# Cross attention in seven-product blocks: values formed with channels on the partitions and turned afterwards, and query tiles of every fourth column

## The chip, the cores and the metric

The kernel runs on one core of one Trainium2 chip. The metric is the device time of one launch in microseconds. TensorE multiplies, and has two rows in the profile: PE for the products and PEld for the loads of their stationary operand. VectorE (DVE), ScalarE (ACT) and GpSimd (POOL) do the elementwise work. SyncE (SP) issues transfers, and GpSimd issues those that add to what lies in SBUF.

## The reference

```
x: (32, 256, 1024)   y = ctx: (32, 256, 1024)   C = 256, N = 1024, float32
x_q = w_qk y (turned), x_k = w_qk x, x_v = w_v x + b_v
energy    = x_q x_k                       # (N queries, N keys)
attention = softmax(energy, over keys)
attention = attention / (1e-7 + attention.sum(over queries))
x_r = x_v attention                       # contracted over the queries' index n
out = x + relu(w_t (x - x_r) + b_t)
```

Since both projections use `w_qk`, the energy is y' (w_qk' w_qk) x. Since `w_t` is applied to `x_r`, the kernel folds it into the values: u = -(w_t w_v) x - w_t b_v, and what is left for the output is w_t x + u attention + b_t.

## The kernel before, in words

All products are float32, and each product of 2 by 2 blocks is done with seven block products instead of eight. A block of the moving operand has 512 columns. The class `Seven` holds the frame: products `p1`, `p5`, `p2`, `p6`, `p3`, `p7`, `p4` in three PSUM banks (`one`, `two`, `three`), with partial sums copied out by ScalarE (`kept`), and four results `c11`, `c12`, `c22`, `c21` made by VectorE (`combine`) or, for `c21`, mostly by ScalarE. Three products lie in the same bank one on another, so `p6` waits for the copy of `p1`, `p7` for the copy `w` of `p6`, and `p4` for `c22`, which reads the bank before.

For each of the 32 batches there are four such objects.

- `Keys`: gx, the matrix w_qk' w_qk times x. Seven products of 512 columns.
- `Values`: u, turned, with n on the partitions and the 256 channels along a row (`ut`). The seven products each are four of 128 columns: a tile of 128 columns of x is stationary and 128 columns of weights move.
- `Energy`, for t = 0 to 3: queries of tile t are stationary (128 columns of y), gx moves (512 columns). The result is a tile of e with the queries on the partitions. ScalarE takes the exponential (`exp`), VectorE adds the normalized rows up in `acc` (`share`).
- `Attention`: the output, po. Seven products with the weights and x (`xpart`), and seven of four each that contract over n (`epart`): tiles of `ut` and of its sums `us` are stationary, normalized e and its sums `et` move.

So 70 products of 512 columns and 28 of 128 make a batch on TensorE. The names of the traces follow: pg, pu, pe and po are the banks of the four objects.

The sums of blocks that the seven products need are made by GpSimd (`gt` from gx, `us` from `ut`, in `factors`) and, for x and y, by transfers that add (`summed`; its three steps are issued on GpSimd's queue, each waiting for the one before). The bias of the values is a transfer too: `Values.bias` adds `uc`, spread over all rows, to the whole of `ut`.

The order on each engine is the order written in the program: `InOrder` chains every instruction of an engine behind the one before, which is why all of them have line 77. SP's queue is in the order of the program too. The loop over the batches runs them overlapped:

1. Energy tiles t = 0 to 3 of batch b. Within t = 0 stands the rest of the batch before: its last product (`before.end()`: `xpart` and `epart` 4), then `before.c21()`, which is an activation on ScalarE into a buffer `z`, an addition on VectorE and a store. On ScalarE that activation stands between the copies of `p5` and `p6` of tile 0. The sums `us` of batch b are started here, then the next x is loaded and, at t = 1 to 3, its sums.
2. While tile 3 drains: `Keys` and `Values` of batch b + 1, the column sums and their inverse `rc`.
3. `Attention` of batch b (`begin`, `run`): VectorE normalizes 16 half tiles of e (`normal`), makes the sums et (`mix`) and the results. `run` ends with `c12`. Then products 7, `c22`, two `put` (relu, addition of x, store), and round again.

The results go through the buffers `z`, of which there are two: `c11`, `c12`, `c22` and `c21` take them in turn, so that `c22` waits for the store of `c11`, and `c21` for the store of `c12`.

Of the kernel before, what the change touches and what calls it, by code (L numbers as in the profile page):

```python
# [9 lines left out]
F32 = mybir.dt.float32  # L10
# [6 lines left out]
def kernel(  # L17
# [48 lines left out]
    class InOrder:  # L66


        def __init__(self, engine):
            self.engine = engine  # L70
            self.last = None
# [37 lines left out]
    def accumulate(into, from_):  # L109
        return pool.dma_start(into, from_, accum_op=ALU.add)  # L110
# [13 lines left out]
    bv = scratch[:, 4, :KC].rearrange("p (k o) -> p k o", o=1)  # L124
    bt = const.tile([P, KC, 1], F32, name="bt")
    nbt = const.tile([P, KC, 1], F32, name="nbt")
    uc = const.tile([P, 1, C], F32, name="uc")
    nc.sync.dma_start(wqk, w_qk.rearrange("(k p) c -> p k c", p=P))
    load("x", 0, KC)
    nc.sync.dma_start(wt, w_t.rearrange("(k p) c -> p k c", p=P))  # L130
# [7 lines left out]
    few = const.tile([P, P], F32, name="few")  # L138
    dve.memset(few, 0.0)
    dve.memset(zeros, 0.0)  # L140
    parts = const.tile([P, NB, NG + 1], F32, name="parts")
    dve.memset(parts[:, :, NG], EPS)
    idle = bank("idle")
# [41 lines left out]
    def value_weights(wtT):  # L185

        pw = [bank(f"pw_{i}") for i in range(KC)]
        for i in range(KC):
            for k in range(KC):
                pe.matmul(  # L190
                    pw[i][:, :C], wv[:, k, ts(i, P)], wtT[:, k, :], start=(k == 0), stop=(k == KC - 1)
                )
        return lefts("wvtT", pw, -1.0)[1]

    bvb = scratch[:, 6, : KC * P].rearrange("p (k c) -> p k c", k=KC)

    def spread_bias():
        for k in range(KC):
            act.activation(bvb[:, k, :], few, AF.Identity, bias=bv[:, k, :], scale=1.0)

    def value_bias(wtT):

        pb = bank("pb")
        for k in range(KC):
            pe.matmul(
                pb[:, :C], bvb[:, k, :], wtT[:, k, :], start=(k == 0), stop=(k == KC - 1)
            )
        act.mul(uc[:, 0, :], pb[:, :C], -1.0)
        act.mul(nbt[:, :, 0], bt[:, :, 0], -1.0)

    up = ctx.enter_context(tc.tile_pool(name="up", bufs=2))
# [7 lines left out]
    def matmul(into, lhs, rhs, onto=False):  # L219
        pe.matmul(into, lhs, rhs, start=not onto, stop=True, skip_group_check=onto)  # L220
# [114 lines left out]
    class Values(Seven):  # L335


        def __init__(self, b, xr):
            super().__init__("u", b)
            self.xr = xr  # L340
            self.ut = up.tile([P, NT, C], F32, tag="ut", name=f"ut_{b}")

        def product(self, into, j, onto=False):
            for t in range(HT):
                pe.matmul(
                    into[:, ts(t, P)],
                    self.xr[j - 1][:, ts(t, P)],
                    u_left[j - 1],
                    start=(t == 0 and not onto),
                    stop=(t == HT - 1),  # L350
                    skip_group_check=True,
                )

        def tiles(self, p):
            return p.rearrange("p (t c) -> p t c", t=HT)

        def block(self, i, h):
            return self.ut[:, h * HT : h * HT + HT, ts(i, P)]

        def combine(self, i, h, in0, in1, op):  # L360
            dve.tensor_tensor(self.block(i, h), self.tiles(in0), self.tiles(in1), op)

        def c21(self):
            act.copy(self.block(1, 0), self.tiles(self.one))

        def bias(self):
            accumulate(self.ut, uc.to_broadcast([P, NT, C]))

        def factors(self):

            us = up.tile([P, 4, HT, P], F32, tag="us", name=f"us_{self.b}")
            s1, s2, s3, s4 = (us[:, j] for j in range(4))
            a11, a12, a21, a22 = (self.block(i, h) for i in range(2) for h in range(2))
            steps = [
                lambda: pool.tensor_tensor(s1, a21, a22, ALU.add),
                lambda: pool.tensor_tensor(s2, s1, a11, ALU.subtract),
                lambda: pool.tensor_tensor(s3, a11, a21, ALU.subtract),
                lambda: pool.tensor_tensor(s4, a12, s2, ALU.subtract),
            ]
            return (a11, a12, s4, a22, s1, s2, s3), steps  # L380

    class Energy(Seven):

# [6 lines left out]
            self.ends = {}  # L390

        def product(self, into, j, onto=False):
            matmul(into, self.rhs[j - 1][:, ts(self.t, P)], self.lhs[j - 1], onto)

        def combine(self, i, h, in0, in1, op):

# [42 lines left out]
    class Attention(Seven):  # L439
# [76 lines left out]
        def run(self, u, before=None):  # L516


            self.normal(0, 0)
            self.normal(1, 0)  # L520
            for j in range(HT // 2):
                self.normal(0, 1, j)
                self.mix(self.t1, self.b11, self.b12, ALU.add, j)
            if u:
                u.c22()
            if before:
                before.put()
                before.c21()
            self.normal(1, 1)
            self.mix(self.t2, self.t1, self.b22, ALU.subtract)  # L530
            self.epart(self.one, 1)
            self.p1s = self.biased(self.one, "p1s", bt[:, 0, :])
            self.epart(self.three, 2)
            self.epart(self.two, 5)
            self.p5s = self.biased(self.two, "p5s", bt[:, 1, :])
            self.xpart(self.one, 6, True)
            if u:
                u.p4()
                u.c21()
                u.c11()  # L540
                u.c12()
            self.c11()
            self.put()
            self.xpart(self.two, 3, True)
            self.epart(self.two, 3, (0, 1))
            self.epart(self.one, 6)
            self.w = self.biased(self.one, "w", nbt[:, 0, :])
            self.mix(self.t3, self.b12, self.b22, ALU.subtract)
            self.mix(self.t4, self.b21, self.t2, ALU.subtract)
            self.epart(self.two, 3, (2,))  # L550
            if u:
                self.epart(self.two, 3, (3,))
                self.c12()

        def end(self):
            self.xpart(self.one, 4, True)
# [57 lines left out]
    g.c11()  # L614
    g.p6()
    wtT, t_left = turned_weights()
    spread_bias()
    g.p3()
    g.c12()
    g.p7()  # L620
    g.c22()
    u_left = value_weights(wtT)
    g.p4()
    g.c21()
    rhs, _ = summed("y", 0)
# [6 lines left out]
    u = Values(0, xr)  # L632
    u.p1()
    u.p5()
    value_bias(wtT)
    u.p2()
    u.c11()
    u.p6()
# [6 lines left out]
    for b in range(B):  # L645
# [3 lines left out]
        for t in range(HT):  # L649
            now = Energy(b, t, lhs, rhs)  # L650
            pair.append(now)
            now.p1()
            if t > 0:
                pair[t - 1].exp(1)
            now.p5()
            if t == 0:
                if b == 0:
                    u.p4()
                    u.c21()
                    u.bias()  # L660
                    xsteps[1]()
                    xsteps[2]()
                elif more:
                    before.end()
                    before.c21()
                    load("x", b + 1)
                e = ep.tile([P, NT, N], F32, tag="e", name=f"e_{b}")
                acc = one.tile([P, N], F32, tag="acc", name=f"acc_{b}")
                ur, usteps = u.factors()
                first = 1 if more else 0  # L670
                for step in usteps[:first] + gsteps + usteps[first:]:
                    step()
            if t > 1:
                pair[t - 2].share(0)
            if t == 0:
                now.p6()
            now.p2()
            now.c11()
            if t == 1:
                pair[0].scale(1)  # L680
            if t > 1:
                pair[t - 1].share(1)
            if t > 0:
                now.p6()
            if t == 1:
                act.activation(acc, e[:, HT, :], AF.Copy, scale=scales[HT])
            if t > 0:
                pair[t - 1].p4()
                pair[t - 1].c21()
                pair[t - 1].exp(0)  # L690
            now.p3()
            now.c12()
            now.p7()
            now.c22()
            if more and b > 0:
                if t == 0:
                    xn, xsteps = summed("x", b + 1)
                else:
                    xsteps[t - 1]()
# [49 lines left out]
        if more:  # L749
            now = Attention(b, xr, ur)  # L750
            now.begin()
            ysteps[0]()
            now.run(un)
            if b + 2 < B:
                now.xpart(now.one, 7, True)
                now.epart(now.one, 7)
                now.c22()
                now.put()
            now.put()
            ysteps[1]()  # L760
            un.bias()
            ysteps[2]()
            before = now
            xr, u = xn, un
        else:
            before.end()
            now.run(None, before)
            now.finish()
# [30 lines left out]
```

## Time and profile before

| | |
|---|---|
| Median of 3 runs | 2141.96 us (2141.42 to 2142.52) |
| The profiled execution | 2142.63 us, its span 2140.9 us |
| PE busy | 2134.6 us (100%), PEld 1058.5 us (49%) |
| DVE busy | 1769.1 us (83%) |
| ACT, POOL busy | 788.5 us (37%), 612.7 us (29%) |
| Chain that ended last | PE 98%, DVE 2% |
| Products of the values (pu) | 1792 rows, 32 x 7 x 4 x 2 |
| Store of a result z | 343 ns on SP, 2.3 us from issue to landing (median) |
| Transfer that adds the bias | 32 x 1024 KB, 9.6 us from issue to landing |

A row of the timeline gives the start, the busy time, the engine, the operation and, in brackets, how long the engine had been idle and what it waited for. A float32 product shows as two rows of MATMUL and two of LDWEIGHTS. The modelled ends of products overlap, so the time of one is the distance of two starts. The batches repeat: the third store of the three of one group leads the next group by the same distance each time, and the stretch from 700 to 780 us of the span is used below for all.

### The profile page before, as it was taken

The numbers are of one execution on the slowest core, as the hardware profiler recorded it, in microseconds if no ns is written. First come the engines' busy times: TensorE is split into PE (matmuls) and PEld (weight loads), VectorE is DVE, ScalarE is ACT, GpSimd is POOL, SyncE is SP. The second block draws the span as 40 slices with busy tenths as digits, with TensorE's granted clock in tenths as the row PEclk, the third lists the DMA queues.
The fourth block names the chain that finished last, engine by engine and source line by source line (L and its number), as shares of the span: only waits on it lengthen the run. The fifth ranks groups of instructions, "written<-read, shape, count | busy, mean of one in ns | idle before, by whom it ended". The sixth has DMA issues, their size and how long they took to land.

```text
span 2140.9 us, 19900 instructions
## 1 busy us (share of the span) xinstructions
PE 2134.6 (100%) x6312; PEld 1058.5 (49%) x6312; DVE 1769.1 (83%) x3119; ACT 788.5 (37%) x1323; POOL 612.7 (29%) x488
## 2 busy tenths in 40 slices
PE   9999999999999999999999999999999999999999
PEld 5455444554445545455544555445554445544453
DVE  5889788898788887879878788778897888978898
ACT  5234443244432344333443234442244422444332
POOL 5322323313233133232232322323223233222320
PEclk9999999999999999999999999999999999999999
DMA  6555665556665556665566655665546655566540
GB/s 176 120 127 119 154 151 123 129 120 150 148 126 135 117 144 148 128 151 106 137 151 138 139 113 128 157 144 126 125 121 153 157 121 125 121 154 148 123 98 30
DMA packets 139048, 282.58 MB, mean 132 GB/s; under 512 B 9152, under 2 KB 42688, under 8 KB 138944
## 3 DMA queue, kind: packets, MB, share of 16 engines
q0 software_dynamic: 75936, 114.83, 34.0%
q1 hardware_dynamic: 63008, 166.48, 23.5%
q8 instruction: 50, 0.82, 0.2%
q14 instruction: 54, 0.44, 0.1%
HBM read 181.67 MB, written 33.55 MB: 101 GB/s over the span
## 4 chain that ended last, share of the span: by engine, by line
PE 98%; DVE 2%; issue 0%; DVEq 0%
PE po L77 44%; PE pe L77 35%; PE pu L77 9%; PE pg L77 9%; DVE e L77 1%; DVE acc L77 0%; PE idle L77 0%; DVE et L77 0%; PE pw L77 0%; DVE z L77 0%; DVE rc L77 0%; DVE sc L77 0%; PE pb L77 0%; DVE ri L77 0%; DVE parts L77 0%
## 5 line engine op out<-in xcount | busy, mean ns | idle before, releaser
L77 PE MATMUL pe<-gt,ys 128*128 128x512 f32 x768 | 392.1, 592 | 0.0
L77 DVE SCALAR_TENSOR_TENSOR e<-e,ri,rc 128x512 f32<-128x512 f32 x512 | 347.3, 745 | 1.1
L77 PE MATMUL po<-et,us 128*128 128x512 f32 x768 | 345.7, 593 | 0.5 <-DVE et L77 0.5
L77 DVE SCALAR_TENSOR_TENSOR acc<-e,ri,acc 128x1024 f32<-128x1024 f32 x224 | 288.6, 1288 | 8.0
L77 PE MATMUL pe<-gx,y 128*128 128x512 f32 x512 | 261.4, 592 | 0.0
L77 PEld LDWEIGHTS po<-et,us 128*128 128x128 f32 x768 | 145.5, 190 | 185.0 <-issue 166.8
L77 PEld LDWEIGHTS pe<-gt,ys 128*128 128x128 f32 x768 | 145.8, 190 | 183.4 <-issue 170.0
L77 PE MATMUL po<-e,ut 128*128 128x512 f32 x512 | 224.9, 592 | 0.0
L77 POOL TENSOR_TENSOR gt<-gx 128x512 f32<-128x512 f32 x64 | 81.6, 1274 | 391.4 <-DVE gx L77 391.4
L77 ACT COPY ep1s<-pe 128x512 f32<-128x512 f32 x128 | 75.0, 586 | 303.4 <-PE pe L77 298.9
L77 ACT ACTIVATE e<-e,nm 128x1024 f32<-128x1024 f32 x128 | 147.1, 1149 | 98.2 <-DVE nm L77 96.7
L77 DVE TENSOR_TENSOR et<-e 128x1024 f32<-128x1024 f32 x128 | 156.8, 1246 | 2.3
L77 PEld LDWEIGHTS po<-e,ut 128*128 128x128 f32 x512 | 97.3, 190 | 122.5 <-issue 106.2
L77 PEld LDWEIGHTS pe<-gx,y 128*128 128x128 f32 x512 | 97.2, 190 | 122.0 <-issue 114.1
L77 POOL TENSOR_TENSOR us<-ut 128x512 f32<-128x512 f32 x64 | 87.0, 1360 | 223.9 <-DMA ut<-uc 223.9
L77 ACT ACTIVATE e<-e,bias 128x1024 f32<-128x1024 f32 x128 | 147.4, 1152 | 1.6 <-DVE bias L77 1.5
L77 POOL DMA_DIRECT2D ut<-uc x32 | 50.5, 1579 | 338.0 <-DVE ut L77 281.1
L77 DVE TENSOR_TENSOR z<-z,x 128x512 f32<-128x512 f32 x31 | 46.3, 1492 | 118.3 <-ACT z L77 118.3
L77 DVE CUSTOM_DVE_ANT_0 e<-pe,ep1s 128x512 f32<-128x512 f32 x128 | 88.1, 688 | 64.2 <-ACT e L77 57.8
L77 PE MATMUL pe<-gx,ys 128*128 128x512 f32 x256 | 130.9, 593 | 0.5 <-DVE nm L77 0.5
L77 PE MATMUL pe<-gt,y 128*128 128x512 f32 x256 | 130.8, 592 | 0.0
L77 PE MATMUL po<-e,us 128*128 128x512 f32 x256 | 120.5, 592 | 0.0
(115 smaller groups left out, 3265.5 us busy)
## 6 DMA issues: line engine op xcount, KB each, us to landing
y<-in_ctx_dram SPq DMA_DIRECT2D x32, 1024.0 KB, 5.0
ut<-uc POOLq DMA_DIRECT2D x32, 1024.0 KB, 9.6
out_dram<-z SPq DMA_DIRECT2D x128, 256.0 KB, 2.3
x<-in_x_dram SPq DMA_DIRECT2D x31, 1024.0 KB, 6.2
xs<-in_x_dram SPq DMA_DIRECT2D x62, 512.0 KB, 4.6
ys<-in_ctx_dram SPq DMA_DIRECT2D x62, 512.0 KB, 4.2
xs<-in_x_dram POOLq DMA_DIRECT2D x31, 512.0 KB, 8.1
xs<-xs POOLq DMA_DIRECT2D x31, 512.0 KB, 5.0
```

Source lines behind the costliest of these rows:

```text
L77: self.last = getattr(self.engine, name)(*args, **kwargs)
```

## The change

The values are made with channels on the partitions: the weights are stationary, and 512 columns of x move, as for the keys. Their bias is now one number for each partition and is added where ScalarE copies partial sums (`bu` and its negative `nbu`); the transfer that added `uc` is gone. `ut` then holds u unturned, and `turn` turns it: VectorE transposes four tiles of 128 x 512 in blocks of 32 x 32, reading every fourth element (n = 4 k + t) and writing every fourth, and sixteen transfers on SP's queue, each of 32 partitions by 4 pieces of 512 bytes, move the blocks to their partitions, back into `ut`. `turn` stands at the end of `run`, behind `c12`.

Since n = 4 k + t, tile t of the values, and so of e, has every fourth n. The queries of an energy tile and the stationary tiles of `ut` and `us` are now read with a step of four elements. `us` is one row of 512 instead of four of 128. On GpSimd a copy of one element, `behind`, comes first in t = 0; it waits for the last sum `et` of the batch before. Then come the two sums `gt`, then the four `us`; before, the first `us` came ahead of the `gt`. The four small products for the bias move from the values of the first batch to the weights.

```diff
     def value_bias(wtT):
 
         pb = bank("pb")
-        for k in range(KC):
-            pe.matmul(
-                pb[:, :C], bvb[:, k, :], wtT[:, k, :], start=(k == 0), stop=(k == KC - 1)
-            )
-        act.mul(uc[:, 0, :], pb[:, :C], -1.0)
+        for i in range(KC):
+            for k in range(KC):
+                pe.matmul(
+                    pb[:, i : i + 1],
+                    wtT[:, k, ts(i, P)],
+                    bv[:, k, :],
+                    start=(k == 0),
+                    stop=(k == KC - 1),
+                )
+        act.mul(nbu[:, :, 0], pb[:, :KC], 1.0)
+        act.mul(bu[:, :, 0], pb[:, :KC], -1.0)
         act.mul(nbt[:, :, 0], bt[:, :, 0], -1.0)
...
     class Values(Seven):
...
-            self.ut = up.tile([P, NT, C], F32, tag="ut", name=f"ut_{b}")
+            self.ut = up.tile([P, KC, MH, MB], F32, tag="ut", name=f"ut_{b}")
 
         def product(self, into, j, onto=False):
-            for t in range(HT):
-                pe.matmul(
-                    into[:, ts(t, P)],
-                    self.xr[j - 1][:, ts(t, P)],
-                    u_left[j - 1],
-                    start=(t == 0 and not onto),
-                    stop=(t == HT - 1),
-                    skip_group_check=True,
-                )
+            matmul(into, u_left[j - 1], self.xr[j - 1], onto)
+
+        def bias(self, tag):
+            return {"p1s": bu[:, 0, :], "w": nbu[:, 0, :], "p5s": bu[:, 1, :]}[tag]
+
+        def kept(self, p, tag):
+            s = temp(tag, f"u{tag}_{self.b}")
+            act.activation(s, p, AF.Identity, bias=self.bias(tag), scale=1.0)
+            return s
...
-            act.copy(self.block(1, 0), self.tiles(self.one))
-
-        def bias(self):
-            accumulate(self.ut, uc.to_broadcast([P, NT, C]))
+            act.activation(self.block(1, 0), self.one, AF.Identity, bias=bu[:, 1, :], scale=1.0)
+
+        def turn(self):
+            turned = one.tile([P, KC * MH, NG, P], F32, tag="turned", name=f"turned_{self.b}")
+            for i in range(KC):
+                for h in range(MH):
+                    dve.transpose(
+                        turned[:, i * MH + h].rearrange("p g (c t) -> p g t c", t=HT),
+                        self.block(i, h).rearrange("p (g k t) -> p g t k", g=NG, t=HT),
+                    )
+            to = self.ut.rearrange("p i h (a c) -> p (i h) a c", a=NG)
+            for a in range(NG):
+                for g in range(NG):
+                    nc.sync.dma_start(to[ts(g, G32), :, a, :], turned[ts(a, G32), :, g, :])
 
         def factors(self):
-            us = up.tile([P, 4, HT, P], F32, tag="us", name=f"us_{self.b}")
+            us = up.tile([P, 4, MB], F32, tag="us", name=f"us_{self.b}")
...
-            return (a11, a12, s4, a22, s1, s2, s3), steps
+            return [
+                f.rearrange("p (c t) -> p t c", t=HT)
+                for f in (a11, a12, s4, a22, s1, s2, s3)
+            ], steps
...
     class Energy(Seven):
...
         def product(self, into, j, onto=False):
-            matmul(into, self.rhs[j - 1][:, ts(self.t, P)], self.lhs[j - 1], onto)
+            queries = self.rhs[j - 1].rearrange("p (k t) -> p t k", t=HT)[:, self.t]
+            matmul(into, queries, self.lhs[j - 1], onto)
...
             if u:
                 self.epart(self.two, 3, (3,))
                 self.c12()
+                u.turn()
...
                 if b == 0:
                     u.p4()
                     u.c21()
-                    u.bias()
+                    u.turn()
...
                 ur, usteps = u.factors()
-                first = 1 if more else 0
-                for step in usteps[:first] + gsteps + usteps[first:]:
+                if before is not None:
+                    pool.tensor_copy(behind, before.t4[:, HT - 1, :1])
+                for step in gsteps + usteps:
                     step()
...
             ysteps[1]()
-            un.bias()
             ysteps[2]()
```

More of the change, by code (lines that the diff above doesn't have):

```diff
@@ L126 @@
     nbt = const.tile([P, KC, 1], F32, name="nbt")
-    uc = const.tile([P, 1, C], F32, name="uc")
+    bu = const.tile([P, KC, 1], F32, name="bu")
+    nbu = const.tile([P, KC, 1], F32, name="nbu")
     nc.sync.dma_start(wqk, w_qk.rearrange("(k p) c -> p k c", p=P))
@@ L140 @@
     dve.memset(zeros, 0.0)
+    behind = const.tile([P, 1], F32, name="behind")
     parts = const.tile([P, NB, NG + 1], F32, name="parts")
@@ L193, in value_weights @@
         return lefts("wvtT", pw, -1.0)[1]
-    bvb = scratch[:, 6, : KC * P].rearrange("p (k c) -> p k c", k=KC)
-    def spread_bias():
-        for k in range(KC):
-            act.activation(bvb[:, k, :], few, AF.Identity, bias=bv[:, k, :], scale=1.0)
     def value_bias(wtT):
         pb = bank("pb")
-        for k in range(KC):
-            pe.matmul(
-                pb[:, :C], bvb[:, k, :], wtT[:, k, :], start=(k == 0), stop=(k == KC - 1)
-            )
-        act.mul(uc[:, 0, :], pb[:, :C], -1.0)
+        for i in range(KC):
[9 more added lines that the diff above has]
+        act.mul(bu[:, :, 0], pb[:, :KC], -1.0)
         act.mul(nbt[:, :, 0], bt[:, :, 0], -1.0)
@@ L354, in tiles @@
-        def tiles(self, p):
-            return p.rearrange("p (t c) -> p t c", t=HT)
+            matmul(into, u_left[j - 1], self.xr[j - 1], onto)
[5 more added lines that the diff above has]
+            return s
         def block(self, i, h):
-            return self.ut[:, h * HT : h * HT + HT, ts(i, P)]
+            return self.ut[:, i, h]
@@ L360, in combine @@
         def combine(self, i, h, in0, in1, op):
-            dve.tensor_tensor(self.block(i, h), self.tiles(in0), self.tiles(in1), op)
+            dve.tensor_tensor(self.block(i, h), in0, in1, op)
         def c21(self):
-            act.copy(self.block(1, 0), self.tiles(self.one))
-        def bias(self):
-            accumulate(self.ut, uc.to_broadcast([P, NT, C]))
+            act.activation(self.block(1, 0), self.one, AF.Identity, bias=bu[:, 1, :], scale=1.0)
[11 more added lines that the diff above has]
+                    nc.sync.dma_start(to[ts(g, G32), :, a, :], turned[ts(a, G32), :, g, :])
@@ L616 @@
     wtT, t_left = turned_weights()
-    spread_bias()
     g.p3()
@@ L622 @@
     u_left = value_weights(wtT)
+    value_bias(wtT)
     g.p4()
@@ L634 @@
     u.p5()
-    value_bias(wtT)
     u.p2()
```

## The prediction

> **What bounds the kernel now.** I read the page's busy shares and the chain that ended last first, then the timeline of one batch, engine by engine, then the groups by shape.
>
> The page says TensorE throughout:
>
> ```profile
> PE 2134.6 (100%) x6312; PEld 1058.5 (49%) x6312; DVE 1769.1 (83%) x3119; ACT 788.5 (37%) x1323; POOL 612.7 (29%) x488
> ...
> PE 98%; DVE 2%; issue 0%; DVEq 0%
> ```
>
> The timeline of TensorE gives the price of each kind:
>
> ```profile
> 1113.38 1.02 PE L77 MATMUL pg<-xs,gs 128*128 128x512 f32 x2
> 1114.23 1.05 PE L77 MATMUL pu<-wvtT,x 128*128 128x128 f32 x8
> 1115.12 1.06 PE L77 MATMUL pu<-wvtTs,xs 128*128 128x128 f32 x8
> 1116.02 1.06 PE L77 MATMUL pu<-wvtT,x 128*128 128x128 f32 x8
> ```
>
> Start to start, a product of 512 columns takes 0.859 us (0.429 a row) and four of 128 take 0.894. A batch is 70 x 0.859 + 7 x 0.894 = 66.39 us. The stores of six batches repeat every 66.34. So TensorE fills the batch, but the other engines run close behind it. That shows around the end of a batch, first on VectorE:
>
> ```profile
> 712.98 0.75 DVE L77 CUSTOM_DVE_ANT_0 e<-pe,zeros,nm 128x512 f32<-128x512 f32 x1
> ...
> 745.76 0.68 DVE L77 TENSOR_TENSOR z<-po,ow 128x512 f32<-128x512 f32 x1
> 749.28 0.69 DVE L77 TENSOR_TENSOR z<-op5s,po 128x512 f32<-128x512 f32 x1 [2.83 <-PE po L77]
> 749.88 2.35 DVE L77 SCALAR_TENSOR_TENSOR z<-z,x 128x512 f32<-128x512 f32 x2
> 756.01 1.58 DVE L77 TENSOR_TENSOR z<-z,x 128x512 f32<-128x512 f32 x1 [3.77 <-ACT z L77]
> ```
>
> The first line is the result of the last energy product, and that product started on PE at 711.92 and ended by 712.78: no slack. From there to c12 (745.76) VectorE has no idle time. Only behind c12 are there 2.83 us. Then ScalarE, TensorE and SP in the same place:
>
> ```profile
> 755.29 0.69 ACT L77 ACTIVATE z<-po,bt 128x512 f32<-128x512 f32 x1 [3.65 <-PE po L77]
> 756.14 0.59 ACT L77 COPY ew<-pe 128x512 f32<-128x512 f32 x1 [0.17 <-PE pe L77]
> ```
>
> ```profile
> 750.79 1.02 PE L77 MATMUL po<-xs,wtT 128*128 128x512 f32 x2
> ...
> 757.66 1.02 PE L77 MATMUL pe<-gt,ys 128*128 128x512 f32 x2
> ```
>
> ```profile
> 741.33 11.27 SPq L489 DMA_DIRECT2D out_dram<-z  x3
> 752.77 0.39 SPq L240 DMA_DIRECT2D xs<-in_x_dram  x1
> 753.22 0.49 SPq L241 DMA_DIRECT2D xs<-in_x_dram  x1
> 757.61 0.34 SPq L489 DMA_DIRECT2D out_dram<-z  x1
> ```
>
> ScalarE's z is `before.c21`. It needs the z buffer of c12, so the landing of c12's store. Behind it on ScalarE stands the copy ew, and p7 of energy tile 0 (PE, 757.66) needs ew. 750.79 is `before.end`, which needs c22.
>
> **Products of the values.** 7 x (0.894 - 0.859) = 0.25 us a batch, 8 us in all, comes off PE where PE is the bound. Once a wait elsewhere sets the period, this gain goes into the wait.
>
> **Transposes.** Four a batch on VectorE, between c12 and c22. The page has no row of 128x512 with steps. The one whole transpose (rc, 128x1024) takes 1.245 us; half is 0.62 in sequence. For the step of four elements the nearest rows are the small moves:
>
> ```profile
> L77 DVE TENSOR_REDUCE parts<-parts 32x32 f32<-32x32 f32 x96 | 19.5, 203 | 1.9
> L77 DVE TENSOR_REDUCE sc<-sc 32x32 f32<-32x32 f32 x32 | 5.6, 175 | 1.1
> ```
>
> `parts` is read and written with a step of five elements, `sc` with none: 28 ns more for 32 elements, which for 512 is 0.45. I take 0.62 + 0.43 = 1.05 each, 4.2 a batch; bounds 0.62 (steps free) and 1.25 (the price of the double size). VectorE's 2.83 us of idle time hide the low value. At 1.05, c22 is done at 746.37 + 4.2 + 0.7 = 751.3 instead of 749.97, past the 750.79 at which `before.end` starts: PE would be held some 0.6 us there. It is not added, since the next wait swallows it.
>
> [...]
>
> **Sixteen transfers on SP.** All need all four transposes, since each moves all four tiles. They stand ahead of the stores of c12 and c22, two loads xs, the store of c21 and the load of x. An issue costs SP 0.34 (a store) plus 0.05 to the next; in a burst the rows above are 0.45 apart and 0.49 long, and in the opening of the kernel 0.51 apart. I take 0.48, 7.7 a batch; bounds 0.39 and 0.51. The bytes are not the limit: the DMA engines are busy five or six tenths, and as 1 MB of plain transfer comes, 1 MB of adding transfer goes.
>
> **The wait that this makes.** Count from the end of c12 at 746.37: transposes 4 x 1.05 + 0.07; to SP 0.03; sixteen issues 7.68; c12's store from issue to landing 2.3 (2.0 to 2.9 in the trace); to ScalarE 0.05; z until ew can start 0.68; ew 0.59; to PE 0.13. Sum 15.73. Before, this way from c12 to p7 of tile 0 was 757.66 - 746.37 = 11.29. So p7 starts 4.44 us late. Nothing gives it back: PE is dense from p7 to the last energy product (21.66 us), VectorE is dense from there to the next c12 (33.39), and 11.29 + 21.66 + 33.39 = 66.34 is the period. The round becomes 66.34 + 4.44 = 70.78. It is run from batch 0 to batch 30, 30 times (the last two batches do not have `end` inside t = 0): + 133.2.
>
> VectorE's own copy of this delay (c21's addition 4.9 us late) has some 3.4 us of gaps in the energy tiles, 1.51 and 0.83 the largest, so PE's delay governs.
>
> **What costs nothing, and its cover.** ScalarE's copies with a bias take 0.69 instead of 0.59 (rows op1s, ep1s); pu's copies wait for PE with 1.8 and 1.2 us idle, and without that cover it is 0.4 a batch. GpSimd loses the bias transfer (1.58 us of issue). Its gt come earlier than before. Its us start when all sixteen have landed, near 760.4 instead of 750.31, so the first adding transfer of xs goes at 766 instead of 758.66 and the second has landed at 779.7, where PE wants it near 778.7 + 4.4. Hidden only because PE is late as well; if PE were on time, it would cost 1 us a batch. The loads xs land by 764, before 766.
>
> **Stationary tiles with a step of four.** 112 of 140 loads a batch. They are 112 ns apart in pu and have 429 ns. In the small moves above, 32 elements would be some 33 ns at the transpose's 1.2 ns or less each, and the steps added 28, so a step about doubles an element; even three times 112 is hidden. Bound below 0; bound above, at five times, 131 ns x 112 x 32 = 470 us. I take 0.
>
> **Sum.** 2142.63 (profiled; span 2140.9 plus 1.7) + 133.2 + 0.7 (turn in batch 0, where VectorE has 2.9 us of gaps for 4.2) - 1 (products outside the round) = 2275.5, say 2275. The profiled execution is 0.7 above the median of the runs; I leave that.
>
> [...] PE would idle about 3.8 us at p7 each batch. [...]
>
> **Rivals.**
> - Faster, 2135: the store of c12 lands in time and all is hidden. Then the gain of 8 us stays. It needs c12's store issued by 753.9, so sixteen issues in 4.8 us (0.30 each) with transposes at 0.62, or 0.20 each at 1.05. No issue row is below 0.34. For it: SP idles much of the batch, and the issues might overlap. 0.10, and 0.02 for no change (within 0.2%, 4 us, what a measurement here can tell).
> - Only c22 is late: transposes long, but the queue short enough. 0.65 us x 30 = 20, so 2163. 0.06.
> - Loads of stationary tiles become the bound: 2400 to 2600. Against it the 317 ns of room a load. 0.06.
> - Likeliest, the queue ahead of c12's store: 0.76. All low bounds (0.62, 0.39, 2.0): way 12.27, 1.0 late, 2172. All high (1.25, 0.51, 2.9): 17.6, 6.3 late, 2332. The opening products are 237 ns apart where later ones are 112, over 3.6 us, so a cold restart can add up to 1.8 us a batch for part of the batches; I stretch the top to 2360.
>
> **Range.** 2160 to 2360 holds the likeliest and the second; it leaves out 0.10 + 0.02 + 0.06. Slower: 0.06 + 0.06 + 0.76 = 0.88.
>
> **What the new profile would show.** Right: PE idle of 3 to 5 us once a batch ahead of `pe<-gt,ys` waiting for ACT ew; ACT z waiting for a DMA; sixteen SP rows near 0.48 apart; STREAM_TRANSPOSE turned near 1.05 us; batches 70 to 71 us apart; pu rows 0.429 apart. Wrong: the transposes near 0.65 and issues under 0.35 (then 2135 to 2185); PEld rows above 0.43 us (then far slower); the idle time elsewhere, ahead of `po<-xs,wtT` or `pg<-xs`, which wait for c22 and for xs.

## The result, and the profile after

The changed kernel takes 2411.93 us (median of 6, 2408.0 to 2415.3) against 2142.06 us before: 1.126 times as long, with an interval of 1.1245 to 1.1274. The forecast was slower, at 2275 us within 2160 to 2360. The sign and the mechanism held, the size did not: twice the predicted loss.

The page of the changed kernel: the busy times, then the chain that ended last.

```profile
PE 2201.5 (91%) x4972; PEld 1362.9 (56%) x4972; DVE 1864.0 (77%) x3247; ACT 797.6 (33%) x1322; POOL 555.6 (23%) x487
...
PE 70%; SPq 12%; DVE 11%; DMA 3%; issue 3%; ACT 2%; DVEq 0%; ACTq 0%
```

PE is idle for a tenth of the span, and SP's queue (SPq), of which the chain before had nothing, now makes 12% of it. The waits (who waited for what, us in total, times, longest):

```profile
ACT z L77 <- DMA out_dram<-z: 357.6, 30, 12.4
...
PE pe L77 <- ACT ew L77: 196.4, 30, 7.0
```

Thirty times ScalarE's z waits for a store, and PE waits for ew, which stands behind z. One such place, engine by engine (start, busy time, operation, idle time before it). VectorE first:

```profile
912.04 0.68 DVE L77 TENSOR_TENSOR z<-po,ow 128x512 f32<-128x512 f32 x1
912.65 4.13 DVE L77 STREAM_TRANSPOSE turned<-ut 128x512 f32<-128x512 f32 x4
916.67 0.65 DVE L77 TENSOR_TENSOR z<-op5s,po 128x512 f32<-128x512 f32 x1
917.23 1.29 DVE L77 SCALAR_TENSOR_TENSOR z<-z,x 128x512 f32<-128x512 f32 x2
930.64 1.58 DVE L77 TENSOR_TENSOR z<-z,x 128x512 f32<-128x512 f32 x1 [12.12 <-ACT z L77]
```

SP, ScalarE and TensorE:

```profile
916.93 10.24 SPq L380 DMA_DIRECT2D ut<-turned  x16
927.28 1.27 SPq L506 DMA_DIRECT2D out_dram<-z  x2
928.73 0.39 SPq L242 DMA_DIRECT2D xs<-in_x_dram  x1
```

```profile
929.92 0.69 ACT L77 ACTIVATE z<-po,bt 128x512 f32<-128x512 f32 x1 [12.09 <-DMA out_dram<-z]
930.51 0.58 ACT L77 COPY ew<-pe 128x512 f32<-128x512 f32 x1
```

```profile
923.49 1.02 PE L77 MATMUL pe<-gt,y 128*128 128x512 f32 x2
931.23 2.06 PE L77 MATMUL pe<-gt,ys 128*128 128x512 f32 x2 [6.72 <-ACT ew L77]
933.09 1.52 PE L77 MATMUL pe<-gx,y 128*128 128x512 f32 x2
934.45 1.02 PE L77 MATMUL pe<-gt,ys 128*128 128x512 f32 x2
```

VectorE is done with the results of c12 and c22 by 918.5 (917.23 + 1.29), but c12's store is issued at 927.28, behind sixteen transfers; z starts when it has landed, then ew, then p7 at 931.23. Two products then take 1.86 and 1.36 us from start to start, where the next ones take 0.86. The windows of the same stretch (busy times of PE, PEld, DVE, ACT, POOL; then the granted clock of TensorE, the DMA share, GB/s) say why:

```profile
932.00:933.00 1.00, 1.00 (x2) 0.33 (x1) 1.00 (x4) 0.00 (x0) 1.00 (x1) 0.50 0.85 342
...
935.00:936.00 1.00, 1.00 (x4) 0.76 (x3) 0.00 (x0) 1.00 (x2) 1.00 (x1) 1.00 1.06 276
```

Behind the wait TensorE runs at half its clock (0.50 granted) until 934, for some 3 us. The starts of the sixteen transfers are 75.20 us apart from one batch to the next; before, a round was 66.34. That is 8.86 more, times 30 = 266 us: nearly all of the 270. Rounds differ a little: from the first p7 that waits (101.33) to the thirtieth (2285.89) they take 75.33 us on average, 8.99 more, and 30 of these make the 270.

### The profile page after: what moved, and what is told of

Its sections match the earlier page's. It is cut to its first block, busy times and chain, and to the rows that moved or that the text cites. A ratio compares the mean times of both kernels' runs of the same rounds, so it can differ in the third digit from the quotient of the medians.

```text
span 2412.4 us, 18205 instructions
## 1 busy us (share of the span) xinstructions
PE 2201.5 (91%) x4972; PEld 1362.9 (56%) x4972; DVE 1864.0 (77%) x3247; ACT 797.6 (33%) x1322; POOL 555.6 (23%) x487
## 4 chain that ended last, share of the span: by engine, by line
PE 70%; SPq 12%; DVE 11%; DMA 3%; issue 3%; ACT 2%; DVEq 0%; ACTq 0%
PE pe L77 28%; PE po L77 25%; SPq L380 12%; PE pg L77 8%; PE pu L77 8%; DVE turned L77 5%; DVE et L77 3%; DMA out_dram<-z 3%; DVE e L77 1%; DVE z L77 1%; ACT z L77 1%; ACT ew L77 1%; DVE acc L77 0%; PE idle L77 0%; DVEq L77 0%
## 5 line engine op out<-in xcount | busy, mean ns | idle before, releaser
L77 PE MATMUL pe<-gt,ys 128*128 128x512 f32 x768 | 427.1, 640 | 196.4 <-ACT ew L77 196.4
L77 PEld LDWEIGHTS pe<-gt,ys 128*128 128x128 f32 x768 | 235.4, 310 | 323.6 <-POOL us L77 201.6
L77 PE MATMUL po<-et,us 128*128 128x512 f32 x768 | 351.3, 600 | 0.8 <-DVE et L77 0.8
L77 PEld LDWEIGHTS po<-et,us 128*128 128x128 f32 x768 | 234.3, 309 | 105.9 <-DVE et L77 16.8
L77 PE MATMUL pe<-gx,y 128*128 128x512 f32 x512 | 284.2, 639 | 0.0
L77 PEld LDWEIGHTS pe<-gx,y 128*128 128x128 f32 x512 | 159.5, 312 | 88.3 <-issue 35.0
L77 POOL TENSOR_TENSOR us<-ut 128x512 f32<-128x512 f32 x64 | 93.2, 1457 | 443.1 <-DMA ut<-turned 437.8
L77 PEld LDWEIGHTS po<-e,ut 128*128 128x128 f32 x512 | 157.8, 308 | 65.6 <-DVE e L77 7.4
L77 ACT ACTIVATE z<-po,bt 128x512 f32<-128x512 f32 x31 | 21.3, 687 | 365.6 <-DMA out_dram<-z 357.6
L77 DVE STREAM_TRANSPOSE turned<-ut 128x512 f32<-128x512 f32 x128 | 132.7, 1120 | 0.5 <-ACT ut L77 0.5
```

The source lines that it names most:

```text
L77: self.last = getattr(self.engine, name)(*args, **kwargs)
```

## The experiments

Each kernel is the changed one with the edit shown, unless it says otherwise. Since "before" was timed along with each group, ratios are to those runs.

**Three buffers for z.**

```diff
     def temp(tag, name):
-        return cp.tile([P, MB], F32, tag=tag, name=name)
+        p = zp if tag == "z" else cp
+        return p.tile([P, MB], F32, tag=tag, name=name)
...
+    zp = ctx.enter_context(tc.tile_pool(name="zp", bufs=3))
```

> The changed kernel with three buffers for the results z instead of two, so that c21 waits for the store of c11, which stands ahead of the sixteen transfers on SP, and no longer for the store of c12 behind them. Theory (the queue ahead of c12's store sets the round): the 6.9 us of PE idle time ahead of p7 of tile 0 go, and so does the half clock behind them. What is late next: us on GpSimd waits for all sixteen, the first adding transfer of xs goes some 10 us later behind c12 than in the kernel before, the second lands near 36 us behind c12, and p6 of the keys (33.4 us behind c12 before) waits 2 to 3 us for it: a round of 68.5 to 69.2 us, 2200 to 2235 us in all. Rival (the time is lost in the transfers or in the half clock itself, whoever waits): near 2400 us.

Measured: 2351.34 us, 1.098 (1.0963 to 1.0996). The wait ahead of p7 is gone, as expected; but another took its place at twice the expected size and with slow products behind it, so the time is far above the 2200 to 2235 us expected. PE's timeline, then GpSimd's and SP's:

```profile
919.46 1.12 PE L77 MATMUL pg<-xs,gs 128*128 128x512 f32 x2 [0.81 <-DMA xs<-in_x_dram]
...
925.73 2.04 PE L77 MATMUL pg<-xs,gs 128*128 128x512 f32 x2 [4.29 <-DMA xs<-xs]
927.57 1.91 PE L77 MATMUL pg<-x,g 128*128 128x512 f32 x2
```

```profile
903.58 1.28 POOL L77 TENSOR_TENSOR us<-ut 128x512 f32<-128x512 f32 x1 [14.50 <-DMA ut<-turned]
...
912.90 1.22 POOL L77 DMA_DIRECT2D xs<-in_x_dram  x1 [3.24 <-PE pe L77]
919.70 1.22 POOL L77 DMA_DIRECT2D xs<-xs  x1 [5.58 <-DMA xs<-in_x_dram]
```

```profile
891.15 10.53 SPq L382 DMA_DIRECT2D ut<-turned  x16
901.79 2.28 SPq L508 DMA_DIRECT2D out_dram<-z  x3
904.16 0.39 SPq L95 DMA_DIRECT2D x<-in_x_dram  x1
904.73 0.39 SPq L244 DMA_DIRECT2D xs<-in_x_dram  x1
905.17 0.46 SPq L245 DMA_DIRECT2D xs<-in_x_dram  x1
```

p6 of the keys waits for the second adding transfer of xs. The loads of xs stand behind the same sixteen transfers, here even behind the third store and the load of x, since SP's queue is not in the order of the program. (The description above says that it is; but `InOrder` does not chain SP's instructions, and in the kernel before, too, the loads xs at 752.77 stand ahead of c21's store at 757.61, which the program has first.) The row of GpSimd at 912.90 names PE as what it waited for; it adds to the load xs issued at 904.73, 17.9 us behind c12 (886.86), where the loads of the kernel before went 6.4 behind (752.77 - 746.37). When that load landed no row here shows. And this wait, too, is followed by slow products: the four from 925.73 on take 6.37 us instead of 3.44 (granted clock of the launch 0.969). So clearing c12's store alone moves the loss to what comes next behind the sixteen.

**No turn, and one half of turn.** The first kernel drops both calls of `u.turn()`, the second only the loop with `nc.sync.dma_start`.

> The changed kernel without the two calls of turn: no transposes, no transfers, so the values that go into the attention are not turned; all else is as in the change (wide products, bias in the copies, stationary tiles with a step of four, the copy behind, the order on GpSimd). Theory (all the loss comes from turn, the rest is free or a gain): the round is TensorE's 77 x 0.859 = 66.14 us, 2134 us in all (2129 to 2139). Rival (the stationary tiles with a step, or the order on GpSimd, cost time): over 2146 us.

> The changed kernel with the transposes but without the sixteen transfers, so the values are not turned. Theory: c22 comes 4.1 us later behind c12, before.end on PE waits for it, and the way from c12 to before.end is 4.72 us as in the changed kernel against 4.42: a round of 66.6 us, 2145 to 2157 us in all; the transfers alone then make over 250 us. Rival (VectorE's added 4.1 us are what sets the round): over 2200 us.

Measured: 2140.74 us, 0.9993 (0.9983 to 1.0002), and 2156.42 us, 1.0069 (1.0054 to 1.0084). So the transposes in their place cost 16 us, and the transfers the other 255. All the rest together costs nothing, but the 8 us that the wide products should bring are hardly there: one or two us, within the interval of nothing, so that 2140.74 lies just above the 2129 to 2139 expected. pu's rows are as short as forecast. Most of the gain is lost at the rows `po<-et,us`: without turn they are busy for 351.1 us of the launch, before for 345.7, and in one batch eight of them take 3.60 us instead of 3.43. VectorE, which makes et, has no idle time there, so TensorE seems to wait for it; no run tests this by itself.

**The strided queries alone**, in the kernel before.

```diff
-            matmul(into, self.rhs[j - 1][:, ts(self.t, P)], self.lhs[j - 1], onto)
+            queries = self.rhs[j - 1].rearrange("p (k t) -> p t k", t=HT)[:, self.t]
+            matmul(into, queries, self.lhs[j - 1], onto)
```

> The kernel before with one part of the change alone: the queries of an energy tile are every fourth column (the values are left with consecutive ones, so the tiles do not belong together). Theory: a load with a step takes 0.31 us instead of 0.19 and stays under the 0.429 us of a product's row: 2142 us, within 0.2% of before. Rival: the loads with a step take port time from the moving operand or hold the products: slower by more than 4 us.

Measured: 2142.84 us, 1.0006 (0.9996 to 1.0016). The groups of loads, first those with a step, then those without:

```profile
L77 PEld LDWEIGHTS pe<-gx,y 128*128 128x128 f32 x512 | 157.8, 308 | 65.3 <-issue 7.4
...
L77 PEld LDWEIGHTS po<-e,ut 128*128 128x128 f32 x512 | 97.3, 190 | 122.5 <-issue 106.2 <-DVE e L77 16.3
```

118 ns more for a load of 128 columns, and all of it lies under the 0.429 us of a row.

**Products to fill the wait.**

```diff
             now.p3()
             now.c12()
+            if t == 0 and b > 0 and more:
+                fill = bank(f"fill_{b}")
+                for _ in range(6):
+                    matmul(fill, now.rhs[0][:, :P], now.lhs[0])
             now.p7()
```

> The changed kernel with six more products of 512 columns in each batch, into a bank that nobody reads, between p3 and p7 of tile 0, where TensorE waits 6.9 us for ew. They are 5.15 us of work and leave under 2 us of idle time. Theory (the wait is one loss, the half clock behind it another, 1.5 us a batch): p7 starts as late as in the changed kernel but at full clock, 30 x 1.5 = 45 us come back: 2367 us (2355 to 2380), granted clock 1.0. Rival (the slow products behind the wait have another cause): 2412 us or more.

Measured: 2374.51 us, 1.1082 (1.1065 to 1.1098), granted clock 0.999. PE's timeline:

```profile
907.27 5.31 PE L77 MATMUL fill<-gx,y 128*128 128x512 f32 x12
915.09 1.22 PE L77 MATMUL pe<-gt,ys 128*128 128x512 f32 x2 [2.51 <-ACT ew L77]
916.15 1.02 PE L77 MATMUL pe<-gx,y 128*128 128x512 f32 x2
917.01 1.02 PE L77 MATMUL pe<-gt,ys 128*128 128x512 f32 x2
```

360 rows of useless products more (12 in each of 30 batches), and 37 us less: behind the wait products start 1.06 and 0.86 us apart. The slow products behind the wait were the clock, a loss of its own beside the wait. 37 came back and not 45; in half of the batches z now also waits for `fill`. The mean clock of 0.999 is a little short of 1.0: one stretch as long as that of the round shown above (0.50 from about 927.2 to 934.0) takes 0.0014 from a mean over 2369.5 us, so by this estimate the clock fell in about one round of the launch here too, though p7 waits 2.5 us at the longest.

**Eight of the sixteen transfers** (`for g in range(0, NG, 2)`).

> The changed kernel with eight of the sixteen transfers, so half of the values are not turned. Theory (the queue ahead of c12's store sets the round, 0.64 us for each transfer): p7 is 7.29 - 5.12 = 2.2 us late, the wait is too short for the half clock, 2142 + 30 x 2.2 = 2208 us (2192 to 2222). Rival (the landing of the transfers or the work on GpSimd behind them, not their number, sets it): over 2300 us.

Measured: 2211.07 us, 1.0326 (1.0308 to 1.0343), granted clock 1.0. SP and PE:

```profile
910.07 5.10 SPq L380 DMA_DIRECT2D ut<-turned  x8
```

```profile
918.90 1.22 PE L77 MATMUL pe<-gt,ys 128*128 128x512 f32 x2 [1.25 <-ACT ew L77]
919.96 1.02 PE L77 MATMUL pe<-gx,y 128*128 128x512 f32 x2
```

Half the issues take half the time, p7's wait shrinks by 5.5 us, and no half clock follows. That such a wait is too short for it was the author's estimate; it held in this launch, with 1.7 us as the longest wait of p7. Three microseconds from the forecast: the number of transfers ahead of c12's store sets the round.

**What makes an issue take 0.60 us.** Three shapes of the same sixteen transfers of 64 KB: 32 partitions by one piece of 2 KB, 128 partitions by one piece of 512 bytes, and the shape of the change but read from x in DRAM.

> The changed kernel with another shape of the sixteen transfers: 32 partitions by one piece of 2 KB instead of four pieces of 512 bytes, the same 64 KB; the values come to the wrong places. Theory A (an issue costs SP by its pieces, 128 of them 0.60 us): 32 pieces take 0.35 us or less, sixteen 5.6 us instead of 10.2, p7 is some 2.7 us late, too short for the half clock: 2200 to 2245 us. Theory B (any transfer from SBUF to SBUF costs SP 0.6 us): 2412 us.

> The changed kernel with sixteen transfers of 128 partitions by one piece of 512 bytes, so again 128 pieces and 64 KB each; the values come to the wrong places. Theory A (by pieces): an issue stays at 0.60 us and the time at 2412 us. Theory C (the second dimension, or having only 32 partitions, makes the issue long): 0.34 to 0.49 us as the store of 128 pieces, 2210 to 2300 us.

> The changed kernel with the sixteen transfers reading x in DRAM instead of turned, in the same shape of 32 partitions by 4 pieces of 512 bytes, so the values are overwritten with parts of x; they no longer wait for the transposes to be written, only for ut to have been read. Theory B (it is the source in SBUF that makes an issue 0.60 us): 0.35 to 0.50 us an issue, sixteen 2.4 us shorter or more, 2310 to 2350 us. Rival (sixteen issues in a row take 0.60 us each whatever the source): 2405 to 2415 us.

Measured: 2356.6 us, 2339.94 us and 2411.89 us (two runs each). In the sixteen of the change, the middle values over the batches are 0.59 to 0.60 us for an issue and 0.643 from start to start. In the other two shapes from SBUF the shortest issue takes 0.51 (32 pieces) and 0.46 (128 partitions), the middle one 0.59 and 0.60. So neither the pieces nor the partitions explain it. The source does not seem to either: the kernel that reads from DRAM takes the time of the change, as its rival expected. Nor is it the length of the row: the first of the sixteen already takes 0.59 and the second starts 0.64 later, the eight of the kernel with half of them show the same values, and in the opening of the kernel before, ten transfers of other kinds go out in a row, nearly all 0.47 to 0.52 apart. What sets the 0.6 is open. The first two kernels gained, but not by a shorter row (11.06 and 10.51 us for the sixteen against 10.24): each of their transfers needs one tile only, and so the row starts behind the first transpose and not the fourth. Theory A's short wait, which by the author's estimate was too short for the half clock, did not come about: with 32 pieces p7 waits 4.21 us in the round shown, and the two products from there take 1.86 and 1.43 us. VectorE and SP of the kernel with 32 pieces:

```profile
891.20 4.14 DVE L77 STREAM_TRANSPOSE turned<-ut 128x512 f32<-128x512 f32 x4
```

```profile
892.42 11.06 SPq L381 DMA_DIRECT2D ut<-turned  x16
```

**Both halves of turn late.** `turn` is called behind the last `put`, its transfers become a function `move` that is called behind the loads xs of tile 0, and `us` comes at the end of tile 3. A second kernel has `move` and `us` late and the transposes where the change has them.

```diff
             now.put()
+            un.turn()
             ysteps[1]()
...
+            if t == 0:
+                u.move()
+            if t == HT - 1:
+                for step in usteps:
+                    step()
```

> The changed kernel with turn in two halves: the four transposes behind the two put at the end of a batch, where VectorE waits 3.8 us for z, and the sixteen transfers behind the loads xs of tile 0 in the program (14 of the 16 come behind the load of x on SP's queue); us on GpSimd comes behind the third adding transfer of xs. Theory (the transfers and transposes are harmful by their place alone; ut is not read before the attention): neither c12's store, nor c22, nor xs waits any more, and the time is that of the kernel without turn, 2141 us (2135 to 2147). Rival (16 transfers and 4.1 us of transposes a batch cost time wherever they stand): over 2160 us.

> As the kernel with both halves of turn late, but with the transposes in the place that the change gives them, between c12 and c22; three transfers stand ahead of c12's store. Theory (with the queue cleared, only c22 is late): as with the transposes alone, 2156 us (2149 to 2163). Rival: the three transfers ahead of c12's store still set the round, over 2175 us.

Measured: 2177.0 us, 1.0161 (1.0146 to 1.0176), and 2195.14 us, 1.0248 (1.0228 to 1.0267): 235 and 217 of the 270 us are back, but both expectations are missed by 36 and 39 us. In the first, z no longer waits for a store and no wait of PE behind the opening exceeds 1 us. VectorE's acc and GpSimd's us of it:

```profile
785.85 2.35 DVE L77 SCALAR_TENSOR_TENSOR acc<-e,ri,acc 128x1024 f32<-128x1024 f32 x1
...
790.68 2.20 DVE L77 SCALAR_TENSOR_TENSOR acc<-e,ri,acc 128x1024 f32<-128x1024 f32 x1
```

```profile
785.51 1.60 POOL L77 TENSOR_TENSOR us<-ut 128x512 f32<-128x512 f32 x1
787.20 2.14 POOL L77 TENSOR_TENSOR us<-us,ut 128x512 f32<-128x512 f32 x1
789.30 1.26 POOL L77 TENSOR_TENSOR us<-ut 128x512 f32<-128x512 f32 x1
790.53 1.27 POOL L77 TENSOR_TENSOR us<-ut,us 128x512 f32<-128x512 f32 x1
```

An acc alone takes 1.28. Beside us, the two of this batch take 2 us more together; over the launch it is 1.3 a batch. All acc of the launch take 329.8 and 332.9 us in the two kernels against 288.4 without turn: 41 and 45 us, about what both missed by. To test it, the four us were held back by a copy of one element of acc, two behind an acc of tile 3 and two behind the last.

```diff
+                pool.tensor_copy(behind, acc[:, :1])
-                for step in usteps:
+                for step in usteps[:2]:
                     step()
...
         last.share(0)
+        pool.tensor_copy(behind, acc[:, :1])
+        for step in usteps[2:]:
+            step()
         columns(b)
```

> As the kernel with all of turn late (2177 us), with the four us on GpSimd moved out of the way of VectorE's acc: two come behind the acc of tile 3, held back by a copy of one element of acc, and two behind the last acc of the batch, held back in the same way. Theory (in that kernel us runs beside two acc of 128x1024, which take 2.2 and 2.35 us there instead of 1.28, 2 us a batch on a VectorE that is now nearly full): the time is that of the kernel without turn, 2141 us (2135 to 2148). Rival (VectorE is too full with 4.1 us of transposes wherever us runs): 2165 to 2180 us.

Measured: 2153.27 us, 1.0053 (1.0039 to 1.0066). 24 of the 36 us come back, which speaks for us beside acc and against a VectorE that is too full as such. The other 12 are about what acc still takes more, 300.8 us in all, 12.4 more than without turn; that they are the same is not shown. In the batch below an acc still meets the second us:

```profile
780.16 1.69 DVE L77 SCALAR_TENSOR_TENSOR acc<-e,ri,acc 128x1024 f32<-128x1024 f32 x1
```

No version beat the kernel before. With turn hidden altogether, the kernel without turn says what would be left to win: 0.07%, within the interval of nothing.

## Why the prediction was wrong, point by point

- **The wait.** Right in every link, which the chain of waits, eight transfers and three buffers for z confirm: c12's store behind the sixteen, z, ew, p7, thirty rounds. From the end of c12 to p7 the round shown has 931.23 - 912.65 = 18.58 us, the thirty have 18.41 on average; predicted 15.73, before 11.29.
- **The issues on SP: the term that failed first.** 0.48 each was taken from pairs and single transfers of other kinds, with 0.51 as the upper bound from the opening. The new transfers go out 0.643 apart. From the first of them to c12's store it is 10.40 us on average instead of 7.68: 2.7 a round, 82 us in all, and as much as the whole way was missed by. It is not the number in the row, since the first already takes 0.59; the chain of the round shown:

```profile
912.73 4.06 DVE turned L77 x4
916.93 0.59 SPq L380
...
917.57 0.59 SPq L380
...
927.28 2.48 DMA out_dram<-z
```

No row of the trace before showed a transfer of this kind, so the prices of others gave no bound. (The store's 2.48 us to landing belong to this round; over the launch the median is 2.3, as predicted.)
- **The half clock: the second term.** The sum held nothing for it, only the top of the range did, as an estimate from the slow products of the opening. No run before the change shows what follows a wait like the 3.8 us that were expected: behind its opening, the longest wait of PE in the kernel before is 0.5 us. In the change, behind the wait, the products lost 1.50 us in the round shown, and between 1.50 and 3.14 in the thirty, 1.86 on average: 56 us. (The rows `pe<-gt,ys` and `pe<-gx,y` are busy for 711.3 us of the launch instead of 653.5, 58 more; with eight transfers, at full clock, the first product behind the wait takes 1.06 us instead of 0.86, which is 6 us in thirty rounds, so by this estimate some of the 58 would come without the half clock too.) The wait for p7 was 6.33 to 7.04 us instead of 3.8, and the granted clock was 0.50 behind it in every round.
- **The sum.** 133 us were predicted for the thirty rounds, 270 measured; 82 from the issues and 56 from the slow products make 138 for the 137 between.
- **The transposes.** Right: 1.05 each in sequence predicted from the small moves, 1.00 in sequence measured (1.12 as the length of a single row). c22 is late as predicted and the wait in it is small, 0.22 us; alone it costs 16 us, where "some 0.6 us" a batch would be 18.
- **The stationary tiles.** Right: 0.308 instead of 0.190, hidden. (A batch has 154 loads, not 140; 112 of them have a step.) The rival of a load that becomes the bound falls.
- **The products of the values.** Their duration was right (0.859 for four of 128 columns' 0.894), the gain of 8 us was not: without turn only 1 or 2 show. The rival "faster, 2135" could not have been reached even with everything hidden: the kernel without turn takes 2140.74.
- **The adding transfers of xs.** Their lateness was seen, but "1 us a batch if PE were on time" was too little. The first of them was to go 766 - 746.37 = 19.6 us behind c12; with three buffers it went 912.90 - 886.86 = 26.0 behind it. With z out of the way they cost more than 6 us of the round, slow products included (a wait of 4.28 us on average, and 2.93 lost in slow products in the round shown).

## What to carry to other kernels

A queue in order hands its delay to all that stand behind (here c12's store, done by 918.5 and issued at 927.28), and the harmful one may be a single store whose buffer somebody needs; list what is behind a new burst on its queue, and who waits for each. Price a transfer by rows of its own kind: the spacing of other transfers (0.45 to 0.51) was no upper bound for these (0.64). Where TensorE is full, a wait has a second price when the clock falls behind it (here 1.86 us a round), and an engine that runs just behind it may take over what a shorter product frees (here all but one or two of 8 us came to nothing; that VectorE took them is not shown by itself).

## What the runs showed of the hardware

- Transfers of 64 KB close behind one another cost SP 0.64 us each from start to start, in rows of sixteen (10.24 us) or eight (5.10). The middle issue takes 0.59 to 0.60 us in three shapes, the shortest 0.59 (the change), 0.51 (32 pieces) and 0.46 (128 partitions); a single store of 256 KB takes 0.34. Why is open.
- TensorE's granted clock was 0.50 behind each of the thirty waits of the change, of 6.33 to 7.04 us. Behind the waits shown of 6.72, 4.29, 4.21 and 3.63 us (the change, three buffers, 32 pieces, 128 partitions) two to four products were slow, and these launches have a mean granted clock of 0.956, 0.969, 0.967 and 0.971. Behind waits of 2.51 and 1.25 (fill, eight transfers) the first product took 1.06 us and the next ones 0.86, with means of 0.999 and 1.0. No round shown has a wait between 2.51 and 3.63, and the 0.999 of fill is short of 1.0, so no limit is read from this.
- A step of four float32 (16 bytes) is not free here: a load of 128 columns goes from 190 to 308 ns, a transpose of 512 columns takes 1.12 us where half of the one of 1024 without steps is 0.62.
- VectorE's acc beside GpSimd's sums us: 2.20 and 2.35 us instead of 1.28. The transposes were not longer beside GpSimd's gt (1.120 us on average in the change, 1.124 in the kernel with both halves late, where gt runs earlier).
